# Loading the second image into the gather buffers at the start, and writing the first gather table ahead of the first offset convolutions

## The chip, the cores and the metric

The kernel runs on one core of a Trainium2 chip. The time is what the device takes for one execution, in microseconds (us); the kernel before was run five times, and its time is the median. The profile is that of one more execution.

## What is computed

The input `x` is 8 images of 256 channels and 64 x 64 pixels, in float32. Two layers follow one another, each added to its own input.

```
x = x + _L0_conv_ref(_gn(x), ...)   # layer 0
x = x + _L1_conv_ref(_gn(x), ...)   # layer 1
```

`_gn` is a group normalisation: 32 groups of 8 channels, mean and variance over the group's channels and all pixels of one image, so no pixel of an image can be normalised before the whole image has been seen.

Layer 0 is a local attention with 4 heads over the 3 x 3 neighbourhood of each pixel. `q`, `k` and `v` are 1 x 1 convolutions; the nine logits of a pixel go through a softmax; a second set of nine weights is generated from the input by a 1 x 1 convolution; both sets weigh the nine `v` of the neighbourhood, and a 1 x 1 projection ends the layer.

Layer 1 is a modulated deformable convolution of 3 x 3 taps. A 3 x 3 convolution with 27 outputs gives, for each pixel and tap, two offsets and a mask. Each tap then samples the image at a position that depends on the data, as a weighted sum of the four pixels around it:

```
v = samp(y0, x0) * ((1 - ly) * (1 - lx))[:, None] + ... + samp(y0 + 1, x0 + 1) * (ly * lx)[:, None]
v = v * mask[:, None]
return jnp.einsum('bckhw,ock->bohw', v, w.reshape(w.shape[0], C, KK))
```

## The kernel before

**Tiles.** An image lies in on-chip memory as `image`, 128 partitions by 2 channel halves by 4096 pixels. It is worked on in 8 chunks of 8 rows (512 pixels). There is room for one such image, so the next image takes its place chunk by chunk.

**The two halves of the work.** The first half of an image is called its front: `attention(b)` (line 614), which is layer 0, and then `prepare(b, gn)` (line 738), which gets layer 1 ready. `prepare` does three things. `flat(c)` (line 746) normalises a chunk on ACT into two `z` tiles, and `to_table(c)` (line 760) transposes them on PE, copies them to a `ts` tile on ACT, and writes them with four DMAs of SP's queue (lines 785 and 788) to a table in device memory, whose entry for a pixel holds that pixel and the one below it. `normed(..)` (line 243) normalises a chunk on DVE into one of three `xn` buffers with a halo row above and below, and `Offsets` (line 797) runs the offset convolution on it: 40 matmuls on PE (line 816) and one ACT copy `om` (line 825). `turned` (line 836, called through `turn`) transposes the result and sums it on DVE, and `positions` (line 862) turns two chunks' results into table indices `idx` and corner weights `wt`, by one sigmoid on ACT and 11 small DVE operations.

The second half is the deformable convolution itself, in 72 slots per image (8 chunks times 9 taps). `gather` (line 1030) fetches table entries into `g` buffers with an indirect DMA of POOL's queue, four per slot; `scale` and `sum_corners` (lines 1044 and 1055) weigh and add the four corners, one on ACT and three on DVE; `transposes` and `product` (lines 1083 and 1097) turn the sums and multiply them with `w_conv` on PE.

**Order.** The order on PE, ACT, DVE and POOL is the order in which the program issues the instructions; each of these engines works its list strictly in that order. SP's list is ordered by a planner. The front is a generator that yields after each step; an image's front has 144 steps. The front of image 0 runs alone, at the start. Twelve steps of `attention(1)` are then issued between the first 16 gathers, and from there on the slots of image b and the steps of the front of image b + 1 alternate.

**The next image.** In `prepare(b)`, `next_normed` (line 926) loads chunk c of image b + 1 into `image` once chunk c of image b isn't needed any more (`load_chunk`, lines 88 to 90; through ACT's queue when b is 0, else through SP's). `first_stats(b + 1, c)` (line 288) takes the statistics of that chunk with two `bn_stats` on DVE, and with the last chunk `Norm` combines them (line 186). `attention(b + 1)` begins with `gn.means()` and `gn.ready()` (lines 188 and 199): two tiny matmuls on PE with four and two small DVE operations and a square root on ACT behind them.

**Buffers.** `gp` is the pool of ten `g` buffers of 4 KB per partition. Before the first gather, four of them hold start-up data (`w_qkv` twice, `w_kgT`, `zero`). The `ts` tiles use three buffers in turn, the `z` tiles of two chunks fit at a time, and all matmul results of the front share four PSUM buffers in turn (`psum_a`, line 176).

Of the kernel before, what the change touches and what calls it, by code (L numbers as in the profile page):

```python
# [9 lines left out]
F32 = mybir.dt.float32  # L10
# [7 lines left out]
P = 128  # L18
# [9 lines left out]
KK = 9  # L28
# [28 lines left out]
def preact_kernel(ctx: ExitStack, tc: tile.TileContext, a: dict, out: bass.AP):  # L57
# [30 lines left out]
    def load_chunk(b, c, queue=nc.sync):  # L88
        s = slice(c * N, (c + 1) * N)
        queue.dma_start(image[:, :, s], sources[b][:, :, s])  # L90

    def const_tile(name, shape, queue=nc.scalar):
        t = const.tile(shape, F32, tag=name, name=name)
        queue.dma_start(t, a[name])
        return t
# [68 lines left out]
            nc.sync.dma_start(t[o : o + n], zero[:n, :ES])  # L164

    w_conv = const_tile("w_conv", [P, NT, KK, C], nc.sync)

    p1 = ctx.enter_context(tc.tile_pool(name="p1", bufs=1))
    p2 = ctx.enter_context(tc.tile_pool(name="p2", bufs=2))
# [119 lines left out]
    def first_stats(b, c):  # L289
        if c == 0:  # L290
            stats0[b] = p2.tile([P, NT, NC, 6], F32, tag="stats0", name=f"stats0_{b}")
        for ct in range(NT):
            nc.vector.bn_stats(
                stats0[b][:, ct, c, :], image[:, ct, c * N : (c + 1) * N]
            )
        if c == NC - 1:
            norm0[b] = Norm(stats0[b], f"0_{b}")
# [316 lines left out]
    def attention(b):  # L614

        xt = image
        first = b == 0
        jobs, due[:] = due[:], []
        gn = norm0[b]
        gn.means()  # L620
        stats = p2.tile([P, NT, NC, 6], F32, tag="stats", name=f"stats1_{b}")
        yield None
        gn = gn.ready()
        yield None
        xn = normed(xt, gn, 0, 2)
        for job in jobs[:1]:
            job()
        yield None
        d = added = None
        for c in range(NC):  # L630
            if c != 1:
                a_ = Attention(b, c, xn, stats)
                a_.q(0)
                if added:
                    added.second_stats()
                if c in (2, 5, 6, 7):
                    yield None
                a_.q(1)
                yield None if c == 4 else "quiet"
            else:  # L640
                a_ = follows
            ahead_of = c + 1 < NC
            at = 2 * (c % 2)
            a_.k(0)
            if ahead_of:
                xn = normed(xt, gn, c + 1, at, cts=(0,))
            yield None if ahead_of else "quiet"
            a_.k(1)
            if ahead_of:
                normed(xt, gn, c + 1, at, cts=(1,))  # L650
            yield None if ahead_of else "quiet"
            if d and not first:
                d.keys(0)
            a_.products(0)
            for job in jobs[c - 1 : c] * (c in (2, 3)):
                job()
            yield None if c in (2, 3) else "quiet"
            a_.generated()
            a_.masked(0)
            yield None  # L660
            a_.products(1)
            a_.turned()
            yield "quiet"
            if d:
                d.weighted(0)
            else:
                a_.v(0)
            a_.masked(1)
            a_.summed()
            yield None  # L670
            a_.logits_1()
            a_.carry_k()
            if d:
                d.keys(1)
                d.carry_v()
                yield None
                a_.v(0)
                a_.logits_2()
                a_.softmax_1()
                yield None  # L680
                d.weighted(1)
                a_.twisted()
            else:
                a_.v(1)
                a_.logits_2()
# [12 lines left out]
            yield None  # L698
            if d:
                d.add(0, d.project(0))  # L700
                yield None
            a_.weights()
            if d:
                d.add(1, d.project(1))
                added = d
            yield None
            a_.spread_weights()
            if first:
                a_.keys(0)
# [24 lines left out]
        yield None  # L734
        gn.ready()
        yield gn.gn

    def prepare(b, gn):
# [187 lines left out]
        def next_normed(c):  # L926
            xn = normed(xt, gn, c, c % 3, (c - 1) % 3)
            if c > NC - 4:
                flat(c)
            if more and c == 1:  # L930
                load_chunk(b + 1, 0, nc.sync if b else nc.scalar)
            if more:
                load_chunk(b + 1, c, nc.sync if b else nc.scalar)
            return xn

        o, pairs = None, {}
# [1 line left out]
        def turn(o):  # L938
            pairs[o.c // 2] = o.turned(o.c % 2)
# [8 lines left out]
            }.get((c, part), [c + 1] if part and c < NC - 4 else []):  # L948
                xn[n] = next_normed(n)

        for c in range(NC - 2):
            to_table(c)
            if o:
                turn(o)
            if c == 2:
                positions(0, pairs[0], 2)
            if c <= NC - 4:
                flat(c + 1)
            normed_at(c, 0)
# [7 lines left out]
        to_table(NC - 2)  # L967
        six = Offsets(NC - 2, xn[NC - 2])
        if more:
            first_stats(b + 1, NC - 3)  # L970
        yield
        to_table(NC - 1)
        turn(o)
        if more:
            first_stats(b + 1, NC - 2)
        yield
        six.part(0, 6)
        positions(2, pairs[1], 2)
        yield
        six.part(6, 12)  # L980
        if more:
            first_stats(b + 1, NC - 1)
        o = Offsets(NC - 1, xn[NC - 1])
        yield
        six.part(12, KK * NT)
        if not more:
            yield
            turn(six)
# [294 lines left out]
```

## Time and profile before

| | |
|---|---|
| median of 5 runs | 4601.97 us (4597.69 to 4606.31) |
| the profiled execution | 4606.75 us, of which the profile's span is 4605.0 us |
| PE busy | 4487.5 us, 97% of the span |
| DVE busy | 4129.4 us, 90% |
| POOL, ACT busy | 2678.4 us, 2529.8 us |
| DMA | 1412.46 MB, mean 307 GB/s |
| mean granted PE clock | 0.991 |

A line of the timeline gives the start, the length, the engine, the line of the kernel, the operation, what it writes and reads, and how many such instructions were merged; in brackets stands the idle time of the engine before it and what ended that. Lines with SPq or ACTq are DMA issues in the queue of that engine. A line of the windows gives, for each engine, the busy time in that stretch and the number of instructions in brackets, and after them the granted PE clock, the share of the DMA engines that was busy, and the GB/s moved.

### The profile page before, as it was taken

Reading aid. Unit: us, or ns where it says so; the run is one execution under the profiler, and the core shown is the slowest. Engines: PE = TensorE matmul, PEld = TensorE weight load, DVE = VectorE, ACT = ScalarE, POOL = GpSimd, SP = SyncE. Lnnn points to the kernel's source line nnn. Section 1 sums busy time; section 2 is a strip of 40 time slices with the busy share of each in tenths; the row PEclk is TensorE's granted clock in tenths of the full one; section 3 lists DMA queues with packets and bytes.
Section 4 is the critical chain, followed back from the end, with each engine's and each line's share of the span. In section 5 each row is a group of like instructions: output and inputs, shape, how many; then the busy total and the mean of one; then the engine's idle time right before and its main releaser. Section 6 shows DMA issues by size and latency. Waiting matters only on the chain.

```text
span 4605.0 us, 77588 instructions
## 1 busy us (share of the span) xinstructions
PE 4487.5 (97%) x25344; PEld 2328.6 (51%) x25344; DVE 4129.4 (90%) x10184; ACT 2529.8 (55%) x5283; POOL 2678.4 (58%) x2841
## 2 busy tenths in 40 slices
PE   8989999999999999999999999999999999998888
PEld 4545555555545555455554555545555555544444
DVE  5679998999999999999999999999998999988887
ACT  3355556555565555655555555555556555564554
POOL 0035655556555665555655565555655556568887
PEclk9999999999999999999999999999999999999999
DMA  3078889888898888988899888998889888898998
GB/s 107 24 244 303 307 313 359 319 297 308 311 380 297 295 312 312 380 305 296 311 323 359 307 300 308 345 331 304 309 312 361 319 289 294 301 346 333 363 363 322
DMA packets 445761, 1412.46 MB, mean 307 GB/s; under 512 B 46430, under 2 KB 63070, under 8 KB 445228
## 3 DMA queue, kind: packets, MB, share of 16 engines
q0 software_dynamic: 331776, 1208.11, 73.9%
q1 hardware_dynamic: 109388, 191.85, 11.5%
q10 hardware_dynamic: 4192, 7.55, 0.5%
q8 instruction: 199, 3.26, 0.3%
q14 instruction: 206, 1.69, 0.1%
HBM read 1275.97 MB, written 131.36 MB: 306 GB/s over the span
## 4 chain that ended last, share of the span: by engine, by line
PE 83%; DMA 8%; DVE 6%; ACT 1%; issue 1%; POOL 1%; SPq 0%; ACTq 0%; DVEq 0%; POOLq 0%
PE po L1115 37%; PE pt L1090 10%; DMA g<-table,idx 6%; PE psk L344 5%; PE proj L589 5%; PE psv L344 5%; PE psq L313 5%; PE om L816 4%; DVE s L1060 4%; PE av L576 3%; PE vk L558 3%; PE qk L387 2%; PE wk L535 2%; DMA x<-in_x_dram 2%; PE gen L430 1%
## 5 line engine op out<-in xcount | busy, mean ns | idle before, releaser
L1036 POOL DMA_INDIRECT g<-table,idx x2304 | 2574.2, 1117 | 1751.6 <-DVE s L1060 542.4
L1060 DVE SCALAR_TENSOR_TENSOR s<-g,wt,s 128x256 f32<-128x256 f32 x6912 | 2824.4, 477 | 177.9 <-ACT s L1052 171.2
L1115 PE MATMUL po<-vt,w_conv 128*128 128x512 f32 x4608 | 2197.9, 602 | 0.0
L1052 ACT ACTIVATE s<-g,wt 128x256 f32<-128x256 f32 x2304 | 1059.4, 510 | 268.2 <-DMA g<-table,idx 230.8
L1115 PEld LDWEIGHTS po<-vt,w_conv 128*128 128x128 f32 x4608 | 813.2, 192 | 771.8 <-issue 762.0
L1093 ACT COPY vt<-pt 128x512 f32<-128x512 f32 x1152 | 616.3, 588 | 373.6 <-PE pt L1090 372.8
L1090 PE MATMUL pt<-ident,s 128*128 128x128 f32 x4608 | 651.3, 279 | 57.2 <-ACT vt L1093 28.5
L1090 PEld LDWEIGHTS pt<-ident,s 128*128 128x128 f32 x4608 | 523.3, 142 | 332.2 <-issue 145.5
L816 PE MATMUL om<-xn,w_off 128*32 128x512 f32 (+1 forms) x2560 | 273.7, 555 | 0.5 <-DVE xn L263 0.5
L344 PE MATMUL psv<-xn,w_qkvT 128*128 128x512 f32 (+1 forms) x576 | 248.5, 558 | 0.9 <-DVE qk L400 0.9
L344 PE MATMUL psk<-xn,w_qkvT 128*128 128x512 f32 (+1 forms) x576 | 248.3, 560 | 0.0
L313 PE MATMUL psq<-xn,w_qkvT 128*128 128x512 f32 x512 | 242.8, 605 | 2.8 <-issue 2.5
L589 PE MATMUL proj<-acc,w_projT 128*128 128x512 f32 x512 | 239.5, 593 | 0.7 <-ACT acc L583 0.7
L321 ACT COPY q<-psq 128x512 f32<-128x512 f32 x128 | 75.0, 586 | 250.3 <-PE psq L313 249.5
L355 ACT COPY k<-psk 128x512 f32<-128x512 f32 (+1 forms) x144 | 79.1, 551 | 202.4 <-PE psk L344 202.4
L400 DVE TENSOR_TENSOR qk<-qk,near_k 128x400 f32<-128x400 f32 x256 | 134.1, 565 | 56.7 <-PE qk L387 56.7
L563 ACT COPY vk<-vk 100x512 f32<-100x512 f32 x256 | 138.2, 588 | 80.5 <-PE vk L558 77.0
L816 PEld LDWEIGHTS om<-xn,w_off 128*32 128x32 f32 x2560 | 75.5, 109 | 209.1 <-issue 202.8
L576 PEld LDWEIGHTS av<-wk,vk 100*64 100x64 f32 x4096 | 130.5, 138 | 92.8 <-issue 38.3
L363 ACT COPY v<-psv 128x480 f32<-128x480 f32 (+1 forms) x144 | 75.6, 525 | 184.0 <-PE psv L344 183.7
L543 DVE TENSOR_TENSOR wk<-wk,near 100x512 f32<-100x512 f32 x256 | 158.6, 681 | 14.2 <-PE wk L535 14.2
L344 PEld LDWEIGHTS psk<-xn,w_qkvT 128*128 128x128 f32 x576 | 104.9, 191 | 123.5 <-issue 108.7
(105 smaller groups left out, 3430.8 us busy)
## 6 DMA issues: line engine op xcount, KB each, us to landing
table<-ts SPq DMA_DIRECT2D x128, 384.0 KB, 9.8
g<-table,idx POOLq DMA_INDIRECT x2304, 6.2
x<-x SPq DMA_DIRECT2D x56, 512.0 KB, 7.2
r<-x SPq DMA_DIRECT2D x56, 512.0 KB, 7.5
out_dram<-r SPq DMA_DIRECT2D x56, 512.0 KB, 3.3
x<-in_x_dram SPq DMA_DIRECT2D x53, 512.0 KB, 11.7
table<-ts SPq DMA_DIRECT2D x128, 128.0 KB, 8.9
x<-in_x_dram ACTq DMA_DIRECT2D x11, 512.0 KB, 4.0
```

The source lines that it names most:

```text
L313: nc.tensor.matmul(ps, w_qkvT[:, ct, m * P : (m + 1) * P], window(self.xn, ct, 4), start=(ct == 0), stop=(ct == NT - 1),)
L344: nc.tensor.matmul(ps[:, : (hi - lo) * W], w_qkvT[:, ct, o : o + P], self.xn[:, ct, lo:hi, 1 : W + 1], start=(ct == 0), stop=(ct == NT - 1),)
L543: nc.vector.tensor_mul(wk.rearrange("p (t n) -> p t n", n=T * T), ps[:NK].rearrange("p (t n) -> p t n", n=T * T), near.unsqueeze(1).to_bro ...
L576: nc.tensor.matmul(av[64 * h : 64 * h + 64, g, t * T * T : (t + 1) * T * T], self.vk[:, t, o : o + 64], self.wk[2 * g + h][:, i * n + t * ...
L589: nc.tensor.matmul(ps, w_projT[:, ct, m * P : (m + 1) * P], self.acc[:, ct].rearrange("p (t y x) -> p y t x", y=T, x=T), start=(ct == 0), ...
L816: nc.tensor.matmul(self.ps[32 * g : 32 * g + 32, cols], w_off[:, ct, k, :], window(self.xn, ct, k)[:, ys], start=(n < 4), stop=(tail >= 0),)
L1036: nc.gpsimd.indirect_dma_start(out=g, out_offset=None, in_=tables[b % 2], in_offset=bass.IndirectOffsetOnAxis(ap=found[b, c][0][:, j, k : ...
L1052: nc.scalar.activation(s, g[:, 0:C], AF.Copy, scale=w[:, 0:1])
L1060: nc.vector.scalar_tensor_tensor(s, g[:, q * C : (q + 1) * C], w[:, q : q + 1], s, ALU.mult, ALU.add)
L1090: nc.tensor.transpose(pt[ct][:, j, :], s[:, ct * P : (ct + 1) * P], ident)
L1093: nc.scalar.copy(v[:, ct, :], pt[ct].rearrange("p b n -> p (b n)"))
L1115: nc.tensor.matmul(po[m], w_conv[:, ct, k, m * P : (m + 1) * P], v[:, ct, :], start=(k == 0 and ct == 0), stop=(b + 1 < B and k == KK - 1 ...
```

## The change

Image 1's eight chunks are loaded at the start, after `w_conv`, into eight `g` buffers called `second`, through SP's queue. `first_stats(1, c)` reads them there, one call per chunk of `attention(0)`, after `k(1)` of that chunk; the norm of image 1 is finished in the last chunk of `attention(0)`, its `means()` after the weights and its `ready()` after the spreading of the weights. `attention(1)` finds the norm done. In `prepare(0)`, POOL copies each `second` chunk into `image` when image 0's chunk isn't needed any more; nothing is loaded there. The jobs of `prepare(0)` are issued in a list written out by hand, all in one step, with 16 empty steps after it: `T` is `to_table`, `z` is `flat`, `x` is `normed` with the copy of the chunk before, `O` is the whole offset convolution, `t` is `turn`, `p` is `positions`, and `S` is a third of the offset convolution of chunk 6. All eight table chunks come ahead of the offset convolutions of chunks 4 to 6. For later images the jobs are unchanged.

```diff
     w_conv = const_tile("w_conv", [P, NT, KK, C], nc.sync)
+    second = []
+    for c in range(NC):
+        t = gp.tile([P, NT, N], F32, tag="g", name=f"second{c}")
+        nc.sync.dma_start(t, sources[1][:, :, c * N : (c + 1) * N])
+        second.append(t)
...
             nc.vector.bn_stats(
-                stats0[b][:, ct, c, :], image[:, ct, c * N : (c + 1) * N]
+                stats0[b][:, ct, c, :],
+                second[c][:, ct] if b == 1 else image[:, ct, c * N : (c + 1) * N],
             )
...
-        gn.means()
+        if b != 1:
+            gn.means()
...
-        gn = gn.ready()
+        gn = gn.gn if b == 1 else gn.ready()
...
             a_.k(1)
             if ahead_of:
                 normed(xt, gn, c + 1, at, cts=(1,))
+            if first:
+                first_stats(1, c)
...
             a_.weights()
+            if first and c == NC - 1:
+                norm0[1].means()
...
             a_.spread_weights()
+            if first and c == NC - 1:
+                norm0[1].ready()
...
             if more and c == 1:
-                load_chunk(b + 1, 0, nc.sync if b else nc.scalar)
+                load_chunk(b + 1, 0)
             if more:
-                load_chunk(b + 1, c, nc.sync if b else nc.scalar)
+                load_chunk(b + 1, c)
...
-        for c in range(NC - 2):
+        if b == 0:
+            flat(1)
+            order = (
+                "T0 z2 x1 T1 z3 O0 T2 t z4 x2 O1 T3 t z5 p0 T4 z6 x3 O2 T5 t z7 x4 T6 O3 "
+                "T7 t x5 O4 x6 t O5 x7 t p2 S0 S1 S2"
+            )
+            for job in order.split():
...
+                elif kind == "x":
+                    xn[n] = normed(xt, gn, n, n % 3, (n - 1) % 3)
+                    for m in range(n - 1, n + (n == NC - 1)):
+                        nc.gpsimd.tensor_copy(image[:, :, m * N : (m + 1) * N], second[m])
...
+            o = Offsets(NC - 1, xn[NC - 1])
+            for n in range(2 * NC):
+                yield
+        for c in range((NC - 2) * (b > 0)):
             to_table(c)
```

More of the change, by code (lines that the diff above doesn't have):

```diff
@@ L949, in normed_at @@
                 xn[n] = next_normed(n)
[L951 removed]
+        if b == 0:
[5 more added lines that the diff above has]
+            for job in order.split():
+                kind, n = job[0], int(job[1:] or 0)
+                if kind == "T":
+                    to_table(n)
+                elif kind == "z":
+                    flat(n)
+                elif kind == "x":
+                    xn[n] = normed(xt, gn, n, n % 3, (n - 1) % 3)
+                    for m in range(n - 1, n + (n == NC - 1)):
+                        nc.gpsimd.tensor_copy(image[:, :, m * N : (m + 1) * N], second[m])
+                elif kind == "O":
+                    o = Offsets(n, xn[n])
+                    o.all()
+                elif kind == "t":
+                    turn(o)
+                elif kind == "p":
+                    positions(n, pairs[n // 2], 2)
+                elif n == 0:
+                    six = Offsets(NC - 2, xn[NC - 2])
+                    six.part(0, 6)
+                elif n == 1:
+                    six.part(6, 12)
+                else:
+                    six.part(12, KK * NT)
+            o = Offsets(NC - 1, xn[NC - 1])
+            for n in range(2 * NC):
+                yield
+        for c in range((NC - 2) * (b > 0)):
             to_table(c)
@@ L966, in prepare @@
             yield
[L967 to L985, printed above, removed]
+        if b > 0:
+            to_table(NC - 2)
+            six = Offsets(NC - 2, xn[NC - 2])
+            if more:
+                first_stats(b + 1, NC - 3)
+            yield
+            to_table(NC - 1)
+            turn(o)
+            if more:
+                first_stats(b + 1, NC - 2)
+            yield
+            six.part(0, 6)
+            positions(2, pairs[1], 2)
+            yield
+            six.part(6, 12)
+            if more:
+                first_stats(b + 1, NC - 1)
+            o = Offsets(NC - 1, xn[NC - 1])
+            yield
+            six.part(12, KK * NT)
         if not more:
```

## The prediction

> **What bounds the kernel now.** I first read the windows of three stretches: the start up to the first regular slots, the regular part, and the end.
>
> ```profile
> 0.00:345.00 345.00, 305.70 (x2288) 159.48 (x2288) 217.77 (x471) 137.66 (x269) 42.20 (x45) 0.96 0.39 125
> 345.00:4550.00 4205.00, 4135.40 (x22915) 2147.52 (x22915) 3875.10 (x9608) 2368.18 (x4967) 2601.54 (x2733) 0.99 0.90 322
> 4550.00:4605.00 55.00, 46.44 (x144) 21.60 (x142) 36.55 (x107) 23.93 (x49) 34.67 (x65) 0.97 0.71 271
> ```
>
> The reader is to see PE's column. In the regular part PE is busy 4135.40 of 4205 us, 98%; the change leaves that part's jobs alone, so whatever it does shows as a shift of the point where the slots begin. In the first 345 us PE is busy 305.70 us, so 39.3 us are idle. About 16 us of it lies before the first projection at 24.46 us, when PE waits for inputs and statistics. What is left is what the change can reach, and I went to PE's timeline for it, then to the queues.
>
> ```profile
> 276.94 4.07 PE L816 MATMUL om<-xn,w_off 128*32 128x512 f32 x40
> 283.92 0.35 PE L191 MATMUL gn<-mv,gmat 128*128 128x2 f32 x2 [2.91 <-DVE mv L186]
> 285.21 0.56 PE L202 MATMUL gv<-gnd,gmat 128*128 128x2 f32 x2 [0.93 <-DVE gnd L197]
> ...
> 287.08 5.76 PE L313 MATMUL psq<-xn,w_qkvT 128*128 128x512 f32 x8 [0.36 <-DVE xn L263]
> 292.67 4.49 PE L344 MATMUL psk<-xn,w_qkvT 128*128 128x128 f32 x16
> ...
> 299.28 0.58 PE L387 MATMUL qk<-k,q 64*64 64x100 f32 x16 [1.61 <-ACT k L355]
> ...
> 318.18 0.73 PE L522 MATMUL w<-ident,wts 128*128 128x128 f32 x4 [4.62 <-DVE wts L510]
> ```
>
> Behind the last offset matmuls (276.94, 4.07 us long) PE waits for the second image's norm (2.91, 0.93 and 0.36 us), then for a k copy that sits in ACT's list behind a corner scale that waits for its gather (1.61), and at last 4.62 us for the softmax weights. Between the two starts 287.08 (first projection of image 1) and 318.18 (its weights) lie 31.1 us. The windows add a second price of the norm wait, the clock in the column before the last two:
>
> ```profile
> 284.00:288.00 4.00, 2.71 (x9) 1.83 (x10) 2.51 (x12) 0.26 (x1) 0.00 (x0) 0.56 0.96 238
> 288.00:292.00 4.00, 4.00 (x7) 1.71 (x6) 1.39 (x3) 0.58 (x1) 0.73 (x1) 0.59 0.36 85
> ```
>
> The eight projection matmuls at 287.08 took 5.76 us; the same eight took 3.71 us at 74.85 us, in the steady part of the first front. So the wait costs about 2 us more by the clock.
>
> Then the queues: SP's first table chunk, SP's last table DMA, and POOL's first gather.
>
> ```profile
> 241.53 0.60 SPq L785 DMA_DIRECT2D table<-ts  x1
> 242.19 0.60 SPq L788 DMA_DIRECT2D table<-ts  x1
> 242.84 1.34 SPq L785 DMA_DIRECT2D table<-ts  x1
> 244.23 0.70 SPq L788 DMA_DIRECT2D table<-ts  x1
> ...
> 286.37 0.61 SPq L788 DMA_DIRECT2D table<-ts  x1
> ```
>
> ```profile
> 291.27 1.08 POOL L1036 DMA_INDIRECT g<-table,idx  x1 [284.56 <-issue]
> ```
>
> A chunk's four DMAs occupy SP from 241.53 to 244.93, 3.4 us, when nothing else moves. All eight took until 286.98, 45.5 us, or 5.7 per chunk, because the offset convolutions stand between them and because 4.2 MB of image 1 were loaded through the same DMA engines. The last write lands about 4.3 us after its issue (median of line 788 there), and the first gather starts at 291.27. The table ends the wait for it.
>
> **The change, part by part.**
>
> *Table first.* I walk the lists with the rows of before: a T is 0.95 us on PE and 1.07 on ACT, a z pair 1.52 on ACT, an O 4.0 on PE and 0.69 on ACT, a t 0.6 on PE. Starting as now at 238.43, PE reaches T7 at 266.5; ACT, which also has the sigmoid and its table load (1.28) before T4, ends the copy of T7 at 268.5. SP at 3.4 to 3.5 us per chunk then runs without a gap from T4 on and is done at 272.7; plus 4.3 gives 277 for the first gather instead of 291.27. POOL's copies lie in its list before that gather. A POOL copy isn't in this trace. Below it is bounded by POOL's memset of 128x1320 (3.47 us for three, so 0.9 us for 1024 elements), above by POOL's longest row near here, 3.37 us; I take 1.2, nearest to the memset. Only copies 6 and 7 are late (x7 waits for O4, 272 us): 273 + 2 x 1.2 = 275.4, at worst 280. Both hold before the landing is wanted (first scale at about 290), so by itself this part is worth only what waits for gathers today.
>
> *The list's own price.* In the new list t stands directly behind its O twice (O4, O5) and once behind a T whose ACT copy is late (after O2), so PE waits about 0.9 us for the ACT copy three times: the stage's PE work ends at 282.8 instead of 281.0. DVE then still has the positions (3.2 us) after the last t (279.5) and the first normed chunk of image 1; the projection starts at 283.4. Against 287.08 the norm wait's removal is worth **3.7 us**.
>
> *The start of the slots.* From there I walk to the weights again. At full clock the projections take 3.7 and k 4.4; the first scale stands behind the first k copies, 6.9 us in; from there DVE has no gap: 4 pairs of corner sums (4 x 2.5), two masks (2 x 1.05), and the logits and softmax rows (7.8) end at 26.8. So 26.9 us instead of 31.1: **4.2 us**, of which 2 are the clock and the rest the gather waits. From the weights on, PE and DVE are both full (windows 320 to 420), so the shift stays: 3.7 + 4.2 = 7.9 us gained.
>
> *First statistics in the first front.* 16 `bn_stats` (0.64 us each, 10.2 us in all) move to DVE's list between normed and the first mask. From chunk 1 on DVE idles 5.3 to 6.7 us just there, waiting for PE, so 1.28 us per chunk cost nothing if the data is there; were that cover gone it would be 1.28 per chunk. For chunk 0 the data may not be there:
>
> ```profile
> 27.43 0.59 SPq L94 DMA_DIRECT2D w_conv<-in_w_conv_dram  x1
> ```
>
> ```profile
> 23.95 2.36 DVE L263 TENSOR_SCALAR xn<-x,gn 128x512 f32<-128x512 f32 x6
> 35.75 1.06 DVE L400 TENSOR_TENSOR qk<-qk,near_k 128x400 f32<-128x400 f32 x2 [9.44 <-PE qk L387]
> ```
>
> ```profile
> 28.00:32.00 4.00, 4.00 (x13) 2.10 (x12) 0.00 (x0) 1.36 (x3) 0.00 (x0) 1.00 1.07 317
> 32.00:36.00 4.00, 3.83 (x43) 1.98 (x43) 0.25 (x1) 1.34 (x3) 0.00 (x0) 1.00 1.00 332
> 36.00:40.00 4.00, 4.00 (x48) 2.44 (x45) 3.18 (x6) 1.13 (x3) 0.00 (x0) 1.00 0.45 172
> 40.00:44.00 4.00, 4.00 (x13) 1.96 (x12) 3.76 (x9) 2.87 (x8) 0.00 (x0) 1.00 0.00 0
> ```
>
> `w_conv` is issued at 27.43 and the DMA engines are full until about 38.5 (share 1.07, 1.00, 0.45). `second0` stands behind it. With 2.4 MB ahead at 320 GB/s, its own 0.5 MB, and some 2 us to landing (512 KB landed in 3.7 at the least), it lands between 37.5 and 41. The mask, at 35.75 today, sits behind the statistics in DVE's list, and PE's second half of the products waits for it; from there to the weights DVE has no gap (35.75 to 46.6), so the delay passes on in full: landing + 1.3 - 35.75 = 3.0 to 6.5, and I take **4.7 us** lost. If the load is there by 34.4 it is nothing. Chunk 1 needs `second1` at 53 us, when 4.2 MB have long moved at 350 GB/s.
>
> *The norm in the last chunk.* Two tiny matmuls (0.35 each) and one turn of the four PSUM buffers, which lets the v transposes wait for a DVE product (0.6 us instead of at once): about 1.0 us (0 to 2). Its square root's table load takes the place of the one at 228.87, both in idle ACT time. The eight loads that leave ACT's queue (0.4 us each) had cover there.
>
> **Sum:** -3.7 - 4.2 + 4.7 + 1.0 = -2.2 us on the profiled execution's 4606.75. That one lies 4.8 above the median, so I apply the difference to the median: 4601.97 - 2.2 = 4599.8, forecast **4600**.
>
> *Two rules against it.* The clock: 284 to 292 was granted 0.56 and 0.59 after the wait at 281. The Trainium skill's "TensorE: Matmul & The Clock Gate", Part 1, says an idle window of about 3.4 us halves the clock until a busy one of that length has passed; by that a stall of 4.7 us in chunk 0 costs another 1.7 us (an estimate from that page), and the sum would be -0.5. The row above agrees (2 us), but in chunk 0 PE has room beside DVE, so I leave it out. The port: the Trainium skill's "SBUF — State Buffer", section Who interferes with whom, says a DVE operation in a two-port mode and a POOL operation shut each other out for a whole instruction; eight copies could then block normed. No row here shows a POOL copy; DVE is busy 35 of 60 us from 234 on, so by the rule the sum stays.
>
> **Rivals.**
>
> A, *the early loads cost nothing* (`second0` is issued ahead of the zeroing or `w_conv` and lands before 34.4). For it: SP's list is ordered by a planner, and the zeroing rows already stand out of program order. Against it: `w_conv` is the older job. 4601.97 - 3.7 - 4.2 + 1.0 = 4595; with the gains at their good ends (no PE gaps in the list, 2 us, and one more us at the weights) 4592.
>
> B, *slower: the eight loads land as one batch*. If the eight share the DMA engines evenly, 4.2 MB behind 38.5 us at 350 GB/s end at 50.5. DVE's chunk 0 statistics, hence the mask and PE, then wait until 47 to 52: a loss of 12.5 to 17.5 instead of 4.7, 4607.6 to 4612.6, with 4610 in the middle. It decides from a landing later than 41.4, where the loss eats the 6.9. For it: nothing in the trace shows eight loads in one queue landing one by one under load; the first five at the start landed at 5.8 to 13.1 us after issue. Against it: DVE's statistics there started one after the other (6.58, 9.95, 11.54), which speaks for landing in order.
>
> C, *the table comes no earlier*: chunks still take 5.7 us of SP, the first gather stays at 291, the weights stay within 1 us of today's, and the loss of 4.7 and 1.0 is left: 4607.
>
> **How the numbers follow.** A difference under 0.2% (9.2 us) is about what a measurement of this kernel can't tell from no change. Forecast 0.55 (of it 0.05 faster, 0.03 slower, by the ends of its terms), A 0.22 (0.10 of it faster), B 0.15 (0.10 slower), C 0.08. So faster 0.15, same 0.72, slower 0.13. The range runs from A's good end, 4591 with a us to spare, to short of B's middle, 4609.
>
> **What would show it.** The first gather at 275 to 280 us; no norm matmuls before image 1's projection, which starts near 283 plus the loss of chunk 0; 27 us from it to the weights; the first mask near 40 us with DVE waiting for `second` before it; SP's table DMAs ending near 273 plus that loss. I am wrong if the first mask stays at 36 (A) or goes past 46 (B), if the table still takes 45 us (C), or if the regular part, 4205 us of it, changes length, for which I see no reason.

## The result and the profile after

The changed kernel takes 4601.84 us (median of 25 runs, 4592.28 to 4611.45), the kernel before 4599.89 us (46 runs, 4589.16 to 4606.31). The ratio is 1.0006, with a 95% interval of 1.0001 to 1.0011: slower by 0.5 to 5 us, where a gain of 2.2 us was forecast. The profiled execution took 4606.68 us (before 4606.75), its span is 4604.4 us (4605.0).

Windows of the same three stretches, in the profile of the changed kernel:

```profile
0.00:345.00 345.00, 304.37 (x2279) 159.16 (x2280) 217.72 (x467) 132.46 (x262) 48.91 (x50) 0.96 0.39 122
345.00:4550.00 4205.00, 4136.18 (x22927) 2147.27 (x22926) 3877.74 (x9614) 2369.79 (x4972) 2608.86 (x2737) 0.99 0.90 322
4550.00:4605.00 55.00, 45.57 (x142) 21.40 (x140) 35.66 (x105) 23.08 (x48) 34.22 (x64) 0.97 0.70 267
```

The reader is to see that PE's busy time is what it was in each stretch, to 1.4 us. Nothing large moved; what moved lies in the first 345 us. PE's timeline between the last offset convolution and image 1's weights:

```profile
288.08 4.07 PE L829 MATMUL om<-xn,w_off 128*32 128x512 f32 x40
293.03 0.66 PE L854 MATMUL omt<-ident,om 128*128 128x128 f32 x4 [0.87 <-ACT om L838]
293.52 3.61 PE L319 MATMUL psq<-xn,w_qkvT 128*128 128x512 f32 x8
...
302.13 0.58 PE L393 MATMUL qk<-k,q 64*64 64x100 f32 x16 [0.16 <-ACT k L361]
...
319.82 1.09 PE L528 MATMUL w<-ident,wts 128*128 128x128 f32 x4 [4.62 <-DVE wts L516]
```

The norm's two tiny matmuls and their waits (2.91, 0.93, 0.36 us) are gone from here, and so is the wait of 1.61 us ahead of qk. In the place of the first there is a wait of 0.87 us for ACT's copy of the offsets, which stands ahead of omt (shown once here) three times in the stage. The projection takes 3.61 us instead of 5.76. From it to the weights lie 26.3 us instead of 31.1, and the last wait, 4.62 us for the softmax, is the same to the hundredth. The window there:

```profile
292.00:296.00 4.00, 3.13 (x14) 1.63 (x11) 3.37 (x9) 1.24 (x2) 3.09 (x4) 1.00 0.84 252
```

The clock column, the granted share of PE's full clock, shows 1.00, where it was 0.56 and 0.59. SP's first and last table DMAs and POOL's last copy and first gather:

```profile
250.62 0.60 SPq L798 DMA_DIRECT2D table<-ts  x1
...
253.31 0.70 SPq L801 DMA_DIRECT2D table<-ts  x1
...
285.30 0.61 SPq L801 DMA_DIRECT2D table<-ts  x1
```

```profile
284.51 1.04 POOL L979 COPY x<-second 128x1024 f32<-128x1024 f32 x1 [2.42 <-DVE xn L268]
290.11 1.12 POOL L1083 DMA_INDIRECT g<-table,idx  x1 [4.56 <-issue]
```

The eight chunks hold SP from 250.62 to 285.91 us: 35.3 us, 4.4 per chunk instead of 5.7. The first gather starts 42.6 us after the first table transposes (247.51), where it was 52.8.

And yet the weights come 1.64 us later than before (319.82 against 318.18), since everything from the first front on is late. SP's issues in the first 40 us, DVE's first statistics of `second`, and PE behind them:

```profile
27.11 0.60 SPq L94 DMA_DIRECT2D w_conv<-in_w_conv_dram  x1
28.95 1.52 SPq L164 DMA_DIRECT2D table<-zero  x2
30.52 9.09 SPq L170 DMA_DIRECT2D second<-in_x_dram  x8
```

```profile
40.79 1.29 DVE L298 BATCH_NORM_STATS2 stats<-second 128x6 f32<-128x512 f32 x2 [14.54 <-DMA second<-in_x_dram]
41.99 2.00 DVE L406 TENSOR_TENSOR qk<-qk,near_k 128x400 f32<-128x400 f32 x4
```

```profile
42.61 1.12 PE L455 MATMUL gt<-ident,gs 128*128 128x128 f32 x4 [4.62 <-DVE qk L406]
43.52 6.74 PE L350 MATMUL psv<-xn,w_qkvT 128*128 128x128 f32 x16
```

The loads are issued after the last zeroing rows, `second0` lands at 40.79 us, DVE has waited 14.54 us for it, and the mask stands at 41.99 us instead of 35.75. PE waits 4.62 us for the mask, and the windows show what the clock does then (before, 40 to 44 us were granted 1.00):

```profile
40.00:44.00 4.00, 1.39 (x7) 1.40 (x8) 3.21 (x7) 0.00 (x0) 0.00 (x0) 0.66 1.05 399
44.00:48.00 4.00, 4.00 (x9) 1.93 (x8) 3.83 (x8) 0.45 (x2) 0.00 (x0) 0.50 1.05 386
```

The 16 v matmuls behind it take 6.74 us; before they took 4.49. The first table transposes, which end the first front, come at 247.51 us instead of 238.43: **9.1 us late**, of which 7.4 are won back up to the weights.

### The profile page after: what moved, and what is told of

It reads as the page before. It is cut to its first block, busy times and chain, and to the rows that moved or that the text cites. A ratio compares the mean times of both kernels' runs of the same rounds, so it can differ in the third digit from the quotient of the medians.

```text
span 4604.4 us, 77606 instructions
## 1 busy us (share of the span) xinstructions
PE 4486.1 (97%) x25344; PEld 2327.8 (51%) x25344; DVE 4131.1 (90%) x10184; ACT 2525.3 (55%) x5280; POOL 2692.0 (58%) x2849
## 4 chain that ended last, share of the span: by engine, by line
PE 84%; DMA 9%; DVE 4%; ACT 1%; issue 1%; POOL 1%; SPq 0%; DVEq 0%; ACTq 0%; POOLq 0%
PE po L1162 37%; PE pt L1137 10%; DMA g<-table,idx 6%; PE psv L350 5%; PE psk L350 5%; PE proj L595 5%; PE psq L319 5%; PE om L829 5%; PE av L582 3%; DVE s L1107 3%; PE vk L564 3%; PE qk L393 2%; PE wk L541 2%; DMA x<-in_x_dram 2%; PE gen L436 1%; PE ptab L782 1%
## 5 line engine op out<-in xcount | busy, mean ns | idle before, releaser
L569 ACT COPY vk<-vk 100x512 f32<-100x512 f32 x256 | 138.2, 588 | 78.2 <-PE vk L564 75.2
```

## The experiments

The experiments ran in five groups, each on one chip beside the kernel before, which took from 4600.67 to 4640.89 us in them. So ratios are compared only with the kernel before of the same group, and marks of the head (the time to image 1's first weights) are counted from the start of their own profile.

One measure was needed to read the marks at all. In every profile, that of the kernel before too, the granted clock falls to half here and there in the first front. For each window of 4 us from 28 to 236 us I took 4 x (1 - granted clock) and added them up. These **losses by the clock** come out between 1.7 and 9.9 us, most of them near whole multiples of 1.71: one stretch of half clock each. They differ as much between two profiles of one kernel as between kernels. Taken off, the first front repeats to 1.0 us in four profiles of the changed kernel (7.4 as they stand) and to 2.6 us in four of the kernel before (4.6):

| kernel | first mask | first table transposes | loss by clock | transposes less it | from transposes to weights |
|---|---|---|---|---|---|
| before | 35.75 | 238.43 | 5.1 | 233.4 | 79.8 |
| c1 (before) | 34.85 | 238.07 | 5.4 | 232.6 | 80.4 |
| c4 (before) | 36.54 | 238.71 | 4.0 | 234.8 | 83.1 |
| c6 (before) | 35.20 | 234.09 | 1.9 | 232.2 | 81.8 |
| after | 41.99 | 247.51 | 8.6 | 239.0 | 72.3 |
| c2 (after) | 40.27 | 243.09 | 5.1 | 238.0 | 71.5 |
| c3 (after) | 40.29 | 241.47 | 3.4 | 238.0 | 75.3 |
| c5 (after) | 40.47 | 240.16 | 1.7 | 238.4 | 75.4 |
| e1, e9 (statistics later) | 35.63, 36.02 | 241.42, 236.87 | 8.6, 2.6 | 232.9, 234.2 | 76.7, 75.3 |
| e3 (loads first) | 35.03 | 239.73 | 7.1 | 232.7 | 77.0 |
| e6, e10 (later, turns moved) | 35.77, 35.61 | 239.89, 243.15 | 5.1, 9.9 | 234.8, 233.2 | 69.8, 73.5 |
| e11, e12 (first, turns moved) | 35.53, 36.12 | 238.00, 236.90 | 3.4, 2.6 | 234.6, 234.3 | 74.4, 73.6 |
| e2, e8 (old order of jobs) | 41.63, 42.25 | 242.44, 247.10 | 3.4, 8.6 | 239.0, 238.5 | 78.2, 78.7 |
| e5 (norm late) | 40.79 | 244.74 | 6.8 | 237.9 | 73.7 |
| e7 (turns moved) | 42.77 | 247.21 | 8.6 | 238.7 | 73.8 |
| e4 (loads reversed) | 48.34 | 249.70 | 6.8 | 242.9 | 75.4 |

**What does the wait in chunk 0 cost?** e1 and e9 let the statistics run a chunk late; all else is as in the changed kernel.

```diff
             if first:
-                first_stats(1, c)
+            if first and c:
+                first_stats(1, c - 1)
+            if first and c == NC - 1:
+                first_stats(1, c)
```

> The changed kernel with one edit: the statistics of second chunk c - 1 are taken in chunk c of the first front (chunks 6 and 7 both in the last), so that DVE never stands in front of a load that has not landed. Theory (the wait of chunk 0 for second0 is what turned the gain into a loss): the first mask comes at 35.8 us instead of 41.99, the weights of image 1 start near 319.8 - 6.2 to 8.2 = 312 to 313.5 us, and the time is 6 to 8 us under the changed kernel's, 4 to 5 us under the one before (ratio to before about 0.999). Rival (the first front is longer because DVE and PE carry the statistics and the norm, not because of the load): the first mask moves, but the weights stay within 2 us of 319.8.

> The changed kernel with the statistics one chunk later, again, now beside the changed kernel. Theory (the wait for second0 costs 5 to 8 us and nothing gives it back): the last projection of the first front at 229 to 231 us, the weights of image 1 at 309 to 312 us if the start of the slots takes 26 to 27 us, ratio to before 0.9982 to 0.9992, 4 to 6 us under the changed kernel. Rival (the start of the slots takes 30 us whenever the projection comes early): weights at 315 us or later, ratio above 0.9994.

Measured: ratio 0.9998 (0.9989 to 1.0006) and 0.9997 (0.9985 to 1.0008), less gain than expected. Image 1's weights came at 318.10 and 312.15 us; e1's lie where its rival had them, but with 8.6 us lost by the clock in that front, and both met a standstill told of below. The mask on DVE's timeline in e1, with the wait for PE that it always had:

```profile
35.63 1.05 DVE L406 TENSOR_TENSOR qk<-qk,near_k 128x400 f32<-128x400 f32 x2 [9.68 <-PE qk L393]
```

e3 leaves the statistics and issues the eight loads right after the zero tile is set, ahead of the zeroing of the tables and `w_conv`.

> The changed kernel with the eight early loads issued ahead of the zeroing of the tables and of w_conv, everything else in place. Theory (the wait is for a transfer that stands behind 2.9 MB): second0 lands before 34 us, the first mask comes at 35.8 to 37 us and the weights of image 1 at 312 to 314 us, as with the later statistics. Rival (the statistics themselves, 1.3 us of DVE ahead of the mask, or their norm, cost the time): the mask stays past 38 us.

Measured: ratio 0.9994 (0.9984 to 1.0004), mask at 35.03 us, weights at 316.74 (312 to 314 expected; 7.1 us went by the clock). So the wait can be removed from either end. In the table the seven kernels without it (e1, e9, e3, e6, e10, e11, e12) end the first front at 233.8 us on the mean, less the clock's loss, and the seven that have it and share its norm (after, c2, c3, c5, e2, e7, e8) at 238.5: **the wait costs 4.7 us**, the clock apart. The first number lies 0.6 above the 233.2 of the kernel before; I put that down to the norm in the last chunk, though it is within the spread of the rows.

**Do the loads land one by one?** e4 issues `second0` as the sixth of the eight.

```diff
         t = gp.tile([P, NT, N], F32, tag="g", name=f"second{c}")
-        nc.sync.dma_start(t, sources[1][:, :, c * N : (c + 1) * N])
         second.append(t)
+    for c in (5, 4, 3, 2, 1, 0, 6, 7):
+        nc.sync.dma_start(second[c], sources[1][:, :, c * N : (c + 1) * N])
```

> The changed kernel with the early loads of chunks 0 to 5 issued in reverse order, so that second0 is the sixth. Theory (loads of one queue land one after the other, 1.3 us apart, and DVE's wait passes on in full): second0 lands near 47 us, the first mask near 48, 6 us later than in the changed kernel, and the weights of image 1 near 326 us. Rival (the eight loads share the DMA engines and land as a batch): the mask stays within 2 us of 42.

Measured: DVE's first statistics in e4,

```profile
47.13 1.29 DVE L299 BATCH_NORM_STATS2 stats<-second 128x6 f32<-128x512 f32 x2 [21.20 <-DMA second<-in_x_dram]
```

6.3 us later than the 40.79 of the changed kernel. Were they to land as one batch, the place in the list would not matter. Five places later, `second0` lands 6.3 us later, 1.3 us per load: they land in order.

**What is the table's early place worth, apart from the norm?** e2 and e8 keep the early loads and the early norm, and issue the jobs in the order that the kernel before had.

```diff
-                "T0 z2 x1 T1 z3 O0 T2 t z4 x2 O1 T3 t z5 p0 T4 z6 x3 O2 T5 t z7 x4 T6 O3 "
-                "T7 t x5 O4 x6 t O5 x7 t p2 S0 S1 S2"
+                "T0 O0 x1 T1 t z2 O1 x2 T2 t p0 z3 O2 x3 T3 t z4 O3 x4 "
+                "T4 t x5 z5 O4 x6 z6 T5 t z7 x7 O5 T6 T7 t S0 p2 S1 S2"
```

> The changed kernel with the job list of the first prepare put back in the old order (offsets of a chunk behind its table chunk), the early loads, statistics and norm kept. Theory (the table's place is worth little, since the first gathers wait for nothing once it is 5 us earlier): PE's gaps of 0.9 us behind the last offset convolutions go, the projection of image 1 starts 2 to 3 us earlier than 293.5, the first gather comes near 295, its landing is wanted near 297 and comes near 301, and the weights start between 319 and 323 us, so the time is within 2 us of the changed kernel's. Rival (the table ahead of the offsets is what carries the gain at the start of the slots): weights past 324 us, the time 5 us or more above the changed kernel's.

> The changed kernel with the first prepare's jobs in the old order, again, now beside the changed kernel. Theory (the gathers are late again, but only by a few us): the first gather 2 to 4 us after the projection of image 1, ACT's first scales waiting 4 to 7 us for them, the stretch from the first table transposes to the weights 2 to 4 us longer than in the changed kernel (74 to 76 us), ratio to the changed kernel 1.0004 to 1.001. Rival (the first showing, 35.7 us from the projection to the weights, was the slow chip): the stretch is as long as in the changed kernel.

Measured: ratio 1.0017 (1.0008 to 1.0026) and 1.0015 (1.0005 to 1.0024); e2's weights came at 320.66 us, as its theory had them, its time as its rival had it. PE's timeline in e2 shows the wait that comes back:

```profile
284.96 3.61 PE L319 MATMUL psq<-xn,w_qkvT 128*128 128x512 f32 x8
...
300.21 0.94 PE L393 MATMUL qk<-k,q 64*64 64x100 f32 x16 [6.81 <-ACT k L361]
```

The k copy on ACT stands behind corner scales that wait for their gathers, which wait for the table. So once the norm is early, the table is what is late next, and without the second part of the change the first part brings less than its wait takes. In time, the early table is worth about 5 us (1.0016 against the 1.0004 to 1.0006 of the whole change, with intervals of 2 to 4 us to either side).

**What is the early norm worth?** e5 puts the norm of image 1 back to the start of `attention(1)`; the statistics stay early. One small tile comes from a pool with two buffers.

> The changed kernel with image 1's norm left where it was, at the start of attention(1); its statistics stay in the first front. Theory (the early norm is worth the chain of tiny operations behind the positions on DVE): the first front is 0.9 us shorter, the projection of image 1 starts 2 to 3 us later after the last offset convolution than in the changed kernel, and runs slower by up to 2 us if the clock drops, so the weights come 1 to 4 us later. Rival (the norm wait is hidden behind other work anyway): the weights come no later than in the changed kernel beside it.

Measured, one execution: 4598.64 us; PE waits 0.93 us for gv and 1.22 for the projection, which comes 47.3 us after the first table transposes (45.2 in c2). That is 2.1 us, of which the early norm gives back some 0.6 in the last chunk (238.5 against 237.9 in the table).

**The list's own gaps.** e7 moves the turns behind matmuls that don't wait (`t` is given its chunk's number, and the offset convolutions are kept by chunk for it), e6 and e10 do so with the statistics a chunk late, e11 and e12 with the loads first.

```diff
+                "T0 z2 x1 T1 z3 O0 T2 t0 z4 x2 O1 T3 t1 z5 p0 T4 z6 x3 O2 T5 T6 t2 z7 x4 O3 "
+                "T7 t3 x5 O4 x6 O5 t4 x7 S0 t5 p2 S1 S2"
...
-                    turn(o)
+                    turn(of[n])
```

> The changed kernel with the turns of the job list moved behind the next piece of PE work; the statistics wait for second0 as in the changed kernel. Theory (the parts add up): the first mask at 40 to 42 us, the last projection of the first front at 233 to 238, the stretch from the first table transposes to the weights of image 1 at 69 to 70 us instead of 71.5 to 72.3, the time 2 us under the changed kernel's (ratio to before 0.9985 to 1.0003). Rival (most of what the version with later statistics and moved turns gained came from the turns): ratio below 0.9985.

> The changed kernel with the statistics one chunk later, and with each turn of the job list moved behind the next piece of PE work, so that PE never waits for the ACT copy of the offsets just convolved. Theory (three gaps of 0.9 us and the wait for chunk 0 are all that the change lost): the three waits for om before omt go, the projection of image 1 starts 2 to 3 us earlier than with the later statistics alone, counted from the first table transposes (46.7 us there, 44 to 45 here), and the time is 5 to 9 us under the one before (ratio 0.998 to 0.999). Rival (the start of the slots is bound by DVE and by the gathers, not by when PE gets there): the projection comes earlier but the weights do not, and the ratio stays at 0.9995 or above.

> The changed kernel with the statistics one chunk later and the turns moved, again. Theory: 0.9978 to 0.9992 of the kernel before on a chip of 4600 us (0.9982 was measured), 0.9985 to 0.9997 on one of 4620 us, if the standstill in the first v projection takes back 3.5 us there. Rival (the first ratio was luck): 0.9995 or above on a chip of 4600 us.

> The changed kernel with the early loads ahead of the zeroing and of w_conv, and the turns moved; the statistics stay in their chunk. Theory (the wait for second0 and PE's gaps are all that is lost): the first mask at 35 to 36 us, the first table transposes at 238 to 240 us, weights 69.5 to 70.5 us later on a chip of 4600 us, the same ratio as the version with later statistics within 0.0006. Rival (the statistics in chunk 0 cost DVE and PE even when the load is there): the table transposes come 1 us or more later than with the later statistics, in executions with the same clock.

> The change with the eight loads ahead of the table's zeroing and the turns moved off the matmuls they wait for, a second time. By the wait in chunk 0 gone (4.8 us) and three gaps of 0.87 us gone it should be 5 to 8 us below the change: 5 to 11 us below the kernel before, ratio 0.9976 to 0.9989; if the 0.9971 of the first time holds, 13 us below. If the gain in the head is lost later, as the rival has it, 0.999 to 1.000. First mask at 35.5, first table transposes 233.7 plus 1.7 for each stretch of half clock, 72 to 74 us from there to the weights.

Measured: e7 1.0000 (0.9990 to 1.0009), e6 0.9982 (0.9973 to 0.9991), e10 0.9991 (0.9980 to 1.0001), e11 0.9971 (0.9958 to 0.9983), e12 0.9982 (0.9970 to 0.9995). PE's timeline in e6, at the end of the stage:

```profile
278.16 0.66 PE L856 MATMUL omt<-ident,om 128*128 128x128 f32 x4
...
282.82 0.66 PE L856 MATMUL omt<-ident,om 128*128 128x128 f32 x4 [0.87 <-ACT om L840]
283.31 3.68 PE L319 MATMUL psq<-xn,w_qkvT 128*128 128x512 f32 x8
```

Of the three waits of 0.87 us one is left. Without the wait in chunk 0 this version is faster than the kernel before, in three of four comparisons with an interval that ends below 1, and so than the changed one at 1.0004 to 1.0006; e7, which keeps the wait, is level with the kernel before.

**The kernels unchanged, once more.** c1, c4 and c6 are the kernel before, c2, c3 and c5 the changed one, in the groups of the other runs.

> The kernel before, unchanged, for a profile beside the others on the same chip. Theory (the start of the slots takes about 3.5 us longer on some chips or executions, whatever the kernel, because PE and DVE stand without an instruction there): from the projection of image 1 to its weights 31.1 us become 33 to 36 us if the others of this chip show 30 us, and stay at 31 if they show 26. Rival (the 30 us in the first four experiments come from their edits): 31 us here, and 26 us in the changed kernel beside it.

> The changed kernel, unchanged, for a profile beside the others on the same chip. Theory (chance of the chip or the execution, as above): the first mask again at 41 to 42.5 us; from the projection of image 1 to its weights 29 to 31 us if the others of this chip show that; no drop of the clock near 106 us, which only the first profile had, so the last projection of the first front comes at 233 to 237 us, not at 238.00. Rival (the drop at 106 us belongs to the change): it is there again, and the projection comes at 238.

> The changed kernel, unchanged, timed beside the three others of this call. Theory (7 to 9 us gained between the first table transposes and the weights of image 1, 5 to 9 us lost in the first front, the spread coming from when the clock drops): ratio to before 0.9990 to 1.0008. Rival (the shift of the head is kept at the good end, as in the second profile): ratio 0.9985 to 0.9992.

> The kernel before, unchanged, for a profile. On the chips where the kernel before takes about 4620 us the changed kernel stood still for some 3.5 us in the first v projection of image 1 (30 us from projection to weights instead of 26). Theory (what stands still there is a matter of the chip and would be met by any kernel): on such a chip, 33 to 36 us from the projection of image 1 to its weights here, and 31 us on a chip of 4600 us. Rival (only a kernel whose gathers are ahead meets it, so the gain is smaller there): 31 us here on either chip.

> The changed kernel, unchanged, for a fourth profile. Theory: the first mask at 40 to 42.5 us, the last projection of the first front at 231 to 238 us, the projection of image 1 45.2 to 46 us after the first table transposes, its weights 26 us later on a chip of 4600 us and 30 us later on one of 4620 us. Rival (the spread of the first front is not the clock's): a longer front with no lower clock in it.

> The kernel before, unchanged, for one more profile of it. So far its 28 to 32 us from the first projection of image 1 to that image's first weights were 31.1 us (two profiles where it takes 4600 us) and 33.7 us (one profile where it takes 4640 us). Theory 1: the standstill of some 3.5 us in the first v projections, which every variant of the change shows where the kernel before takes 4618 us or more, is met by the kernel before as well there; then this profile shows 33 to 34 us if the call's level lies above 4610 us, and 31 us if it lies at 4600 us. Theory 2: it is met by the change alone in levels up to about 4625 us; then 31 us here at such a level, and the change loses there some 3.5 us of its gain. In both, the first mask at 34.5 to 36.6 us and, once 1.7 us is taken off for each stretch of half clock, the first table transposes near 233.6 us.

Measured: c1 4597.13, c2 4600.99, c4 4639.56, c5 4635.1 and c6 4638.32 us in one execution each; c3, timed, 1.0004 (0.9995 to 1.0014). They gave the rows of the table, and one more thing. From the first projection of image 1 to its weights the kernel before needs 31.1, 31.1, 33.7 and 33.0 us (the last two where it takes 4640), the changed one 26.3, 26.3, 29.9 and 30.0 (the last two where the kernel before takes 4619 and 4639). There PE stands still in the first v projections, with no releaser that the trace can name ("issue"). In c6, the kernel before:

```profile
298.43 0.61 PE L344 MATMUL psv<-xn,w_qkvT 128*128 128x128 f32 x4
300.74 3.97 PE L344 MATMUL psv<-xn,w_qkvT 128*128 128x512 f32 x8 [1.70 <-issue]
```

Both kernels and the variants meet this standstill where the kernel before takes 4619 us or more, so it is no part of the change; its cause is not settled. It accounts for most of what the last column of e7 (73.8, expected 69 to 70) and e8 (78.7, expected 74 to 76) has too much. Where it appears, the gain between projection and weights is some 3.4 us instead of 4.8.

## Why the prediction was right and wrong

**The norm wait (-3.7).** Right in kind. From the first table transposes to the projection PE now needs 46.0 us (247.51 to 293.52) instead of 48.65: 2.6 us gained. The waits of 0.87 us behind O4 and O5 are there as worked out. The third, behind O2, came to 0.34 us; in its place 0.87 us stand behind the last offset matmuls, where the norm had covered them, and 0.26 us ahead of T6, and these two were not seen ahead.

**The start of the slots (-4.2).** 26.3 us against 26.9 forecast; the gain is 4.8 us. Together with the norm wait 7.4 us (8.9 between c1 and c2), against 7.9.

**The table.** It comes earlier, but not as early as forecast: SP needs 4.4 us per chunk, not 3.5, although hardly anything stands between the chunks. I had taken the first chunk for all: its four DMAs take 3.4 us here too, but both DMAs of line 798, one of which took 0.60 us there, take 1.06 to 1.76 us each in all later chunks. The first gather comes 42.6 us after the first transposes; the forecast was 38.6 (277 less 238.43). The cover was enough: the first k copies and scales are not late. A POOL copy takes 1.04 us (1.2 forecast), and the last ends at 285.55 us, 4.6 us before the first gather. The trace names nothing that ends that wait; the last table DMA, issued at 285.30, would land at about 289.6 by the 4.3 us of before, so the table is the likely one.

**The wait in chunk 0 (+4.7).** `second0` landed at 40.8 us, near the upper end of 37.5 to 41 (39.1 in c2, 41.6 in e7). The mask moved by 6.2 us in the profiled pair, and by 4.8 in c2, c3 and c5 against c1, c4 and c6 (means 40.3 and 35.5). What reaches the end of the first front, at equal clock, is 4.7 us, as forecast.

**The norm in the last chunk (+1.0).** 0.6 us in the table; in the timeline of the profiled pair, 0.8 between the last weights of the first front and its v transposes.

**Rivals.** A, loads that cost nothing, is not this kernel, whose loads stand behind `w_conv`; e3, e11 and e12 make it true and confirm its mechanism; its time of 4595, a ratio of 0.9985, lies just inside e3's interval. B, one batch, falls with e4. C, a table no earlier, falls with SP's rows.

**The clock, which was left out: the step that failed.** "In chunk 0 PE has room beside DVE, so I leave it out" is where the prediction went wrong as far as the runs can show. The wait of 4.62 us was followed by clocks of 0.66 and 0.50 and 2.25 us more for the v matmuls, so the rule that I set aside held. The Trainium skill's "TensorE: Matmul & The Clock Gate", Part 1, says it this way: a window of about 3.4 us without work halves the clock until one with work has passed. Half of 3.4 is 1.7 us, an estimate from that page, and the losses here come in steps of 1.71. Chunk 0 and the start of chunk 1, before and after:

```profile
28.00:72.00 44.00, 41.33 (x312) 21.88 (x313) 23.31 (x46) 17.69 (x38) 0.00 (x0) 0.92 0.23 76
28.00:72.00 44.00, 36.37 (x278) 19.34 (x278) 21.15 (x40) 15.05 (x32) 0.00 (x0) 0.88 0.48 169
```

The kernel before has half clock there too, but later, behind several short waits of PE:

```profile
48.00:52.00 4.00, 3.11 (x17) 2.14 (x18) 2.71 (x5) 0.58 (x1) 0.00 (x0) 0.62 0.00 0
52.00:56.00 4.00, 4.00 (x7) 1.60 (x6) 0.82 (x2) 1.09 (x2) 0.00 (x0) 0.53 0.00 0
```

In windows of 4 us from 28 to 72 the loss is 3.4 us before and 5.1 after. In the eleven profiles without the wait it is 0 to 3.4 there, 2.3 on the mean; in the nine with it 1.7 to 6.8, 4.4 on the mean, and 4.1 without e4, whose wait is longer. From 40 to 44 us eight of the nine show a clock below 1.00, and none of the eleven. So the clock adds 1.7 to 2.0 us to the wait, a difference of means, since single profiles overlap. Over the whole front it is hard to see, 5.9 against 5.1 us, because the stretches behind 72 us fall differently each time. In the profiled pair the loss is 8.6 against 5.1, two stretches more, and these 3.5 us are the whole difference between the 5.7 us that I forecast for the first front and the 9.1 seen there.

**What is left of the sum.** At equal clock the first front moved by +5.1 (the four profiles of each kernel), and what lies behind it, up to the weights, by -7.4 to -8.9 (the clock left in there, as in the forecast's 4.2): -2.3 to -3.8, where -2.2 was forecast. With the clock's 1.7 to 2.0 there remain -0.3 to -2.1; the prediction's own sum would have been -0.5. Nothing taken off, image 1's weights start at 315.9 to 321.8 us in the four profiles of the kernel before (mean 318.6) and at 314.6 to 319.8 in those of the changed one (316.7).

The time moved by +0.5 to +5.0, so 1 to 7 us more are missing. They are not lost in the slots of image 0, for which the prediction's "From the weights on, PE and DVE are both full, so the shift stays" held. Image 1's weights start at 318.18 and 319.82 us, its first table transposes, before and after:

```profile
741.11 1.04 PE L769 MATMUL ptab<-ident,z 128*128 128x128 f32 x8
743.42 1.04 PE L782 MATMUL ptab<-ident,z 128*128 128x128 f32 x8
```

That is 422.9 and 423.6 us, and with the clock's loss taken off in the same way 421.2 in both, as in c1 and c2, e5 and e6: all six profiles where the kernel before takes 4600 us. From there to the end the profiles show, less that loss, 3835 and 3832 us for the kernel before and c1, 3835 and 3837 for the changed one and c2; but where the kernel before takes 4640, 3853 and 3859 for it (c4, c6) and 3852 for the changed one (c5), the other way round. Two profiles of one kernel differ by 2 to 6 us, so no stage can be named. Nor do the variants settle it: e1, e9 and e3, with heads better by 5 to 7 us on the same terms, kept 1 to 3 us at the middle of their intervals, but the intervals of e9 and e3 reach to 7; e6, e10, e11 and e12 kept 4 to 13. **Where these last microseconds come from, and why, stays open.**

## What to carry to other kernels

A load that an in-order engine waits for belongs ahead of every transfer that nobody waits for yet, or its reader behind the work that is due: here a wait of 4.7 us took most of a gain of 7.4 us, and either edit removed it. The price of such a wait on PE is more than its length: the half clock behind it cost another 1.7 to 2.0 us here. When two steps have become equally late, moving one of them shows little: the early loads and norm without the early table (e2, e8) made the kernel slower by 0.15%, and the table brought it back to level. Before two profiles are compared to a few us, take off the time at half clock; it was the larger part of what one pair seemed to show.

## What the runs showed of the hardware

The clock falls to half also where PE hardly waits. Two windows of the changed kernel in the first front, PE's busy time ahead and the clock before the last two columns:

```profile
104.00:108.00 4.00, 4.00 (x16) 1.78 (x13) 3.94 (x7) 1.17 (x2) 0.00 (x0) 0.76 0.35 131
108.00:112.00 4.00, 4.00 (x8) 1.62 (x8) 1.97 (x4) 1.14 (x2) 0.00 (x0) 0.81 0.00 0
```

PE is busy all 8 us, as in the 8 us before, and the eight projection matmuls of that chunk took 5.40 us instead of 3.71. One stretch costs 1.7 us. The rows there:

```profile
102.92 1.95 PE L541 MATMUL wk<-wsb,spread 9*100 9x512 f32 x8
104.81 1.24 PE L564 MATMUL vk<-ident,v 128*100 128x128 f32 x8
106.00 5.40 PE L319 MATMUL psq<-xn,w_qkvT 128*128 128x512 f32 x8
```

Eight of the twenty profiles have one such stretch between 70 and 210 us, the kernel before in c1 (at 98 us) and c4 (at 74 us). The chunk differs, but the place in it does not: all eight begin right behind the eight wk matmuls (9 by 100, where the projection's are 128 by 128) and the eight vk transposes. Whether these small matmuls are the reason, no run shows.

A DVE operation and a POOL copy side by side, and the same operation alone:

```profile
277.91 1.00 DVE L268 TENSOR_SCALAR xn<-x,gn 128x512 f32<-128x512 f32 x2
279.21 1.71 DVE L268 TENSOR_SCALAR xn<-x,gn 128x512 f32<-128x512 f32 x2
279.03 1.17 POOL L979 COPY x<-second 128x1024 f32<-128x1024 f32 x1 [5.85 <-DMA table<-ts]
```

The pair of tensor_scalar operations at 248.28 us, beside the copy at 248.23, took 1.72 us, that at 279.21 beside the copy at 279.03 took 1.71; four pairs away from a copy took 1.00 each. This agrees with the rule of the Trainium skill's "SBUF — State Buffer", Who interferes with whom, at 0.7 us each time; DVE had room both times, as the prediction had it.
